# Layer 0 of a four-layer graph network: the two key blocks of exp added on VectorE ahead of the products with ones, with new rows of turns

## The chip, the cores and the metric

The kernel runs on one core of a Trainium2 chip. The metric is device time in microseconds (us), the median of several executions. The kernel before takes 2660.74 us (median of 3 runs, 2660.52 to 2662.13).

In the profile PE is TensorE's matmul, PEld its weight load, DVE is VectorE, ACT is ScalarE, POOL is GpSimd and SP is SyncE.

## The reference, cut to what matters

64 graphs of 256 nodes with 256 features go through four attention layers, each with a residual and a norm. The change is in layer 0, masked softmax attention with four heads of 64 features:

```python
x, adj                       # (64, 256, 256) each
q, k, v = proj(Wq, bq), proj(Wk, bk), proj(Wv, bv)        # 4 heads of 64
attn = einsum('bhnd,bhmd->bhnm', q, k) * 64 ** -0.5
attn = where(adj == 0, -1e9, attn)
attn = softmax(attn, axis=-1)
out = einsum('bhnm,bhmd->bhnd', attn, v)
out = out.reshape(B, 256, 256) @ Wo.T + bo
x = layernorm(x + layernorm(out) * gamma + beta)
# layer 1: 8 heads of 32 without projections, then a feed-forward of 1024 with gelu
# layers 2 and 3: one head each, edge scores with leaky_relu
```

The kernel works on groups of two graphs, 32 groups in all. It holds exp of the scores with the keys on the partitions, in two blocks of 128 keys. A sum over all keys is a sum over the partitions of both blocks.

## The kernel before: the parts that count here

All groups are Python generators. One turn of a group records the instructions up to its next `yield`; each row of turns is a string of digits that says which group comes next. `FIRST` starts the pipeline, `ORDER` is one period of the steady part (a digit is how many periods ago a group began), and `LAST` ends it. On TensorE the order of the program is kept.

```python
ORDER = "011225334342343542234235432323132121321132121"
...
    att = ctx.enter_context(tc.tile_pool(name="att", bufs=2))
    ps_s = ctx.enter_context(tc.tile_pool(name="ps_s", bufs=2, space=bass.MemoryType.PSUM))
    ps_m = ctx.enter_context(tc.tile_pool(name="ps_m", bufs=4, space=bass.MemoryType.PSUM))
...
    def scores(i, cs, qT, kT, mask, hd, scale, sums=None):
        m = P // hd
        es = []
        for c in cs:
            pss = [ps_s.tile([P, 2, QB * N], F32, name="ps") for _ in range(m // 2)]
            ...  # matmuls of kT and qT into pss
            for ps in pss:
                e = att.tile([P, 2, QB * N], F32, name="e", bufs=6)
                nc.scalar.activation(e, ps, AF.Exp, scale=scale)                      # L605
                if sums is None:      # layer 0
                    nc.vector.tensor_tensor(e, e, mask..., ALU.mult)                  # L607
                else:                 # layer 1: product with the mask, and its sum
                    ... nc.vector.scalar_tensor_tensor(..., accum_out=...)            # L613
                es.append(e)
        return es

    def products(i, cs, v, es, hd, oT, sums, gamma, tally):
        po = ps_m.tile([P, len(cs), N], F32, name="pm")
        ...  # matmuls of v and e into po
        if gamma is not None:
            ...                       # layer 1 ends here
            return
        pz = ps_m.tile([P, N], F32, name="pm")
        for kc in range(QB):
            for h in range(4):
                matmul(pz[32 * h:32 * h + 32, :], ones[:, 0:32], es[h // 2][:, h % 2, kc * N:(kc + 1) * N],
                       start=kc == 0, stop=kc == QB - 1)
        nc.scalar.copy(oT, po)                                                        # L640
        nc.vector.reciprocal(sums, pz)                                                # L641, sums is zs
        nc.scalar.activation(pz, sums, AF.Copy, accum_out=tally[i])                   # L642
```

`attention` runs `scores` of a step, then `products` of the step before. In layer 0 a step is one graph. What comes behind the attention of layer 0:

```python
        def behind(i, oT, rz):
            ...  # rz goes through DRAM into rr, one row for each half of the partitions
            yield
            nc.vector.tensor_tensor(oT, oT, rr, ALU.mult)                             # L730
            yield
            pm = ps_m.tile([P, QB, D], F32, name="pm")
            ...  # matmuls of oT and woT into pm
            nc.vector.tensor_tensor(y[...], pm, over_blocks(bop, QB), ALU.add)        # L737
            ...
```

Beside it, of other groups: `nc.gpsimd.tensor_tensor(x, x, over_blocks(beta0), ALU.add)` (L717) in layer 0, after x has been transposed on TensorE; `transpose(pt[...], e[...], ident)` into a `ps_m` buffer in layer 3 ("ident,qT" in the profile; e has the name qT there), copied by ScalarE (L878); the transposes of xb ahead of the first feed-forward product, copied by ScalarE with scale and bias (L586).

Of the kernel before, what the change touches and what calls it, by code (L numbers as in the profile page):

```python
# [8 lines left out]
F32 = mybir.dt.float32  # L9
# [4 lines left out]
ALU = mybir.AluOpType  # L14
AX = mybir.AxisListType

P = 128
N = 256
# [3 lines left out]
QB = N // P  # L22
# [11 lines left out]
AT_ONCE = 3  # L34


ORDER = "011225334342343542234235432323132121321132121"


FIRST = "000000011000002131100110101000000101"  # L40
LAST = ("001142322312324311231243212120210102100210100031121201213200120132100101010120100010101102"
        "01021000001000010010000")
PREPARE = 2


# [355 lines left out]
def usual_input(ctx: ExitStack, tc: tile.TileContext, a: dict, out: bass.AP, flag: bass.AP):  # L401
# [7 lines left out]
    nc = tc.nc  # L409
# [5 lines left out]
    att = ctx.enter_context(tc.tile_pool(name="att", bufs=2))  # L415
# [14 lines left out]
    ones = const.tile([P, P], F32, name="ones")  # L430
# [88 lines left out]
    def in_order(ins):  # L519

        if on_pe:
            tc.add_manual_dep(ins.ins, on_pe.pop(),
                              mybir.DependencyInfo(mybir.DependencyClass.NoSync, mybir.DependencyReason.DATA),
                              reason="the order of the program")
        on_pe.append(ins.ins.name)

    def matmul(*args, **kw):
        in_order(nc.tensor.matmul(*args, **kw))  # L528
# [60 lines left out]
    def scores(i, cs, qT, kT, mask, hd, scale, sums=None):  # L589

        m = P // hd
        es = []
        for c in cs:
            pss = [ps_s.tile([P, 2, QB * N], F32, name="ps") for _ in range(m // 2)]
            for kc in range(QB):
                for h in range(m):
                    r = h * hd
                    matmul(pss[h // 2][:, h % 2, kc * N:(kc + 1) * N],  # L600
                           kT[r:r + hd, c, i * N + kc * P:i * N + (kc + 1) * P],
                           qT[r:r + hd, c, i * N:(i + 1) * N], start=True, stop=True)
            for ps in pss:
                e = att.tile([P, 2, QB * N], F32, name="e", bufs=6)
                nc.scalar.activation(e, ps, AF.Exp, scale=scale)  # L605
                if sums is None:
                    nc.vector.tensor_tensor(e, e, mask.unsqueeze(1).to_broadcast([P, 2, QB * N]), ALU.mult)  # L607
                else:
                    for h in range(2):
                        for kc in range(QB):  # L610
                            k = slice(kc * N, (kc + 1) * N)
                            j = 2 * len(es) + h
                            nc.vector.scalar_tensor_tensor(e[:, h, k], e[:, h, k], 1.0, mask[:, k], ALU.mult, ALU.mult,  # L613
                                                           accum_out=sums[:, kc, c, j:j + 1])
                es.append(e)
        return es

    def products(i, cs, v, es, hd, oT, sums, gamma, tally):

        m = P // hd
        po = ps_m.tile([P, len(cs), N], F32, name="pm")
        for n, c in enumerate(cs):
            for kc in range(QB):
                for r in range(0, P, 32):
                    h = r // hd
                    e = es[n * (m // 2) + h // 2]
                    matmul(po[r:r + 32, n, :], v[:, i * QB + kc, c * P + r:c * P + r + 32],  # L630
                           e[:, h % 2, kc * N:(kc + 1) * N], start=kc == 0, stop=kc == QB - 1)
        if gamma is not None:
            nc.scalar.activation(oT[:, cs[0], :], po[:, 0, :], AF.Identity, scale=gamma[:, cs[0]:cs[0] + 1])
            return
        pz = ps_m.tile([P, N], F32, name="pm")
        for kc in range(QB):
            for h in range(4):
                matmul(pz[32 * h:32 * h + 32, :], ones[:, 0:32], es[h // 2][:, h % 2, kc * N:(kc + 1) * N],
                       start=kc == 0, stop=kc == QB - 1)
        nc.scalar.copy(oT, po)  # L640
        nc.vector.reciprocal(sums, pz)  # L641
        nc.scalar.activation(pz, sums, AF.Copy, accum_out=tally[i])  # L642

    def attention(qT, kT, v, mask, hd, gamma, behind, tally=None):

        scale = hd ** -0.5
        m = P // hd
        before = sums = None  # L650
        after = []

        def go_on():
            for r in list(after):
                if next(r, END) == END:
                    after.remove(r)

        for i in range(G):
            for cs in ((0, 1),) if m == 2 else ((0,), (1,)):
                if cs[0] == 0 and gamma is not None:  # L660
                    sums = small.tile([P, QB, NC, 4], F32, name="r1")
                es = scores(i, cs, qT, kT, mask[:, i, :], hd, scale, sums)
                if before:
                    products(*before)
                go_on()
                if cs[0] == 0:
                    oT = att.tile([P, NC, N], F32, name="oT")
                    zs = att.tile([P, N], F32, name="zs") if sums is None else sums
                if before and before[1][-1] == NC - 1:
                    after.append(behind(before[0], before[5], before[6]))  # L670
                before = (i, cs, v, es, hd, oT, zs, gamma, tally)
                yield
        products(*before)
        after.append(behind(G - 1, oT, zs))
        yield
        while after:
            go_on()
            yield
# [22 lines left out]
    def layer0(g, x, mask):  # L701
# [20 lines left out]
        def behind(i, oT, rz):  # L722
# [26 lines left out]
            yield  # L749

        yield from attention(qT, kT, v, mask, 64, None, behind, [r_0[:, g * G + i:g * G + i + 1] for i in range(G)])
        return xb, z

    def layer1(xb, z, mask):
# [6 lines left out]
        def behind(i, oT, r):  # L761
# [14 lines left out]
            yield  # L776

        yield from attention(zT, zT, z, mask, 32, gamma1, behind)
        yT = transposed(xb, gamma2, beta2)
        yield  # L780
# [212 lines left out]
    def turn(g):  # L993
        done[g] += 1
        next(groups[g], END)
        if g == 0 and done[0] > PREPARE:
            next(preparing, END)

    for g in FIRST:
        turn(int(g))  # L1000
    for period in range(len(groups)):
        for age in ORDER:
            g = period - int(age)
            if g >= 0:
                due[g] += 1
                if due[g] > done[g]:
                    turn(g)
    for back in LAST:
        turn(len(groups) - 1 - int(back))
# [55 lines left out]
```

## Time and profile before

| what | value |
|---|---|
| time, median of 3 | 2660.74 us |
| span of the profiled execution | 2659.6 us |
| mean granted clock of TensorE | 0.992 |
| instructions | 44925 |
| mean rate of memory traffic | 31 GB/s |
| PE waits in the whole span, behind DVE z (L559) | 8.2 us in 30 waits, longest 0.3 |
| PE waits behind DVE oT (L730) | 8.6 us in 2 waits, longest 7.0 |
| PE waits behind ACT e (L605) at the scores | 6.5 us in 5 waits, longest 4.7 |

A row of the groups names line, engine, operation, output and inputs, shapes and count; then busy time and the mean of one in ns, and the idle time ahead of it with what ended that. "x1024" counts records: an f32 product has two records on TensorE. A row of the timeline gives start and duration in us, and in brackets the idle time ahead of it. Busy times of groups whose instructions run beside each other are the time they cover together.

### The profile page before, as it was taken

How to read it: one execution, taken by the hardware profiler on the slowest of the kernel's cores; microseconds unless marked ns; L12 is line 12 of the kernel's file. 1: busy time of each engine (PE TensorE's matmuls, PEld its weight loads, DVE VectorE, ACT ScalarE, POOL GpSimd, SP SyncE). 2: the span in 40 equal slices, each digit the busy share in tenths (PEclk: the TensorE clock that was granted, in tenths of full speed). 3: DMA queues.
4: the chain of work that ended last, by engine and by line, in shares of the span. 5: the costliest groups of instructions: out<-in, count | busy, mean ns of one | idle time of the engine just before them, and what ended most of it. 6: DMA issues, size and time to landing. Idle time of an engine off the chain costs nothing.

```text
span 2659.6 us, 44925 instructions
## 1 busy us (share of the span) xinstructions
PE 2586.6 (97%) x16648; PEld 1765.4 (66%) x16648; DVE 1967.4 (74%) x6189; ACT 1290.4 (49%) x1995; POOL 586.8 (22%) x1139
## 2 busy tenths in 40 slices
PE   6899999999999999999999999999999999999997
PEld 3467667666667676666676666676676676676665
DVE  4667777777777777777777777777777777777774
ACT  3445544545544445545455444555445455445442
POOL 1112222212222212222222222222222222222121
PEclk8999999999999999999999999999999999999998
DMA  5000011000010100110010110010110001000000
GB/s 155 25 9 29 29 37 30 31 29 29 29 37 28 33 30 26 32 37 26 28 37 25 32 37 25 29 37 21 36 37 25 29 29 29 29 29 17 17 1 25
DMA packets 113729, 83.20 MB, mean 31 GB/s; under 512 B 44256, under 2 KB 113120, under 8 KB 113504
## 3 DMA queue, kind: packets, MB, share of 16 engines
q1 hardware_dynamic: 112144, 79.47, 9.8%
q8 instruction: 134, 2.20, 0.3%
q10 hardware_dynamic: 1360, 0.79, 0.1%
q14 instruction: 91, 0.75, 0.1%
HBM read 54.80 MB, written 17.04 MB: 27 GB/s over the span
## 4 chain that ended last, share of the span: by engine, by line
PE 70%; DVE 17%; POOL 8%; issue 2%; DMA 1%; SPq 1%; ACT 1%; DVEq 0%; POOLq 0%; ACTq 0%
PE pm L528 54%; PE ps L528 10%; PE pm L531 7%; POOL rstd L551 6%; DVE st L544 3%; DVE y L814 2%; DVE y L742 2%; DVE xn L559 2%; POOL ve L547 2%; DVE z L559 2%; DVE mv L545 1%; DVE xb L748 1%; DVE y L741 1%; DVE r L813 1%; POOL ve L549 0%
## 5 line engine op out<-in xcount | busy, mean ns | idle before, releaser
L613 DVE SCALAR_TENSOR_TENSOR e<-e,mask 128x256 f32<-128x256 f32 x1024 | 428.3, 483 | 129.0 <-ACT e L605 129.0
L605 ACT ACTIVATE e<-ps 128x1024 f32<-128x1024 f32 x384 | 372.0, 1019 | 196.6 <-PE ps L528 176.3
L528 PE MATMUL pm<-L_gnn_W,hT 128*128 128x256 f32 x2048 | 463.2, 380 | 0.0
L528 PE MATMUL pm<-xT,L_gnn_W 128*128 128x512 f32 x1024 | 456.4, 594 | 0.0
L528 PEld LDWEIGHTS pm<-L_gnn_W,hT 128*128 128x128 f32 x2048 | 385.3, 191 | 48.9 <-issue 1.1
L786 ACT ACTIVATE hT<-pm,b 128x512 f32<-128x512 f32 x256 | 176.7, 690 | 409.8 <-PE pm L528 409.8
L528 PEld LDWEIGHTS pm<-xT,L_gnn_W 128*128 128x128 f32 x1024 | 193.0, 191 | 204.0 <-issue 199.5
L544 DVE BATCH_NORM_STATS2 st<-y 128x6 f32<-128x256 f32 x768 | 301.1, 408 | 6.7
L551 POOL TENSOR_TENSOR rstd<-ve,mhalf 128x2 f32<-128x2 f32 (+1 forms) x384 | 297.7, 775 | 26.6
L559 DVE TENSOR_SCALAR xn<-y,mv,rstd 128x256 f32<-128x256 f32 x384 | 142.2, 412 | 177.3 <-POOL rstd L551 177.3
L547 POOL TENSOR_SCALAR ve<-mv 128x2 f32<-128x2 f32 x384 | 98.7, 257 | 750.4 <-DVE mv L545 749.9
L772 POOL TENSOR_TENSOR both<-y,xb 128x512 f32<-128x512 f32 x64 | 81.3, 1270 | 757.2 <-DVE y L771 757.2
L607 DVE TENSOR_TENSOR e<-e,mask 128x1024 f32<-128x1024 f32 x128 | 151.0, 1220 | 18.5 <-ACT e L605 18.5
L528 PE MATMUL ps<-xT 32*128 32x256 f32 x2048 | 147.5, 401 | 2.2 <-ACT e L605 1.3
L586 ACT ACTIVATE xT<-pm,beta,gamma 128x512 f32<-128x512 f32 x128 | 92.2, 769 | 108.4 <-PE pm L531 108.3
L528 PE MATMUL pm<-e,z 128*32 128x256 f32 x2048 | 141.5, 385 | 0.4
L528 PEld LDWEIGHTS ps<-xT 32*128 32x128 f32 x2048 | 93.1, 184 | 73.3 <-issue 67.1
L528 PE MATMUL ps<-qT,kT 64*128 64x256 f32 x1024 | 129.2, 392 | 5.2 <-ACT e L605 5.2
L528 PE MATMUL pm<-e,v 128*32 128x256 f32 x2048 | 126.4, 387 | 6.3 <-DVE e L607 6.3
L528 PE MATMUL pm<-L_gnn_WoT,oT 128*128 128x256 f32 x512 | 119.3, 387 | 8.6 <-DVE oT L730 8.6
L528 PE MATMUL pm<-xT,L_gnn_WqT 128*128 128x512 f32 x256 | 121.2, 617 | 3.5 <-ACT xT L584 3.5
L814 DVE SCALAR_TENSOR_TENSOR y<-pm,r,xn 128x256 f32<-128x256 f32 x256 | 120.8, 473 | 2.5
(136 smaller groups left out, 4053.7 us busy)
## 6 DMA issues: line engine op xcount, KB each, us to landing
x<-in_x SPq DMA_DIRECT2D x32, 512.0 KB
adj<-in_adj SPq DMA_DIRECT2D x32, 512.0 KB
rr<-lines SPq DMA_DIRECT2D x128, 128.0 KB
out<-xn SPq DMA_DIRECT2D x31, 512.0 KB
adjT<-adjb SPq DMA_TRANSPOSE x128
L_gnn_W<-in_L_gnn_W SPq DMA_DIRECT2D x2, 1024.0 KB
lines<-zs SPq DMA_DIRECT2D x64, 4.0 KB
out<-xn SPq DMA_DIRECT2D x2, 256.0 KB
```

The costliest lines, as they stand in the source:

```text
L528: in_order(nc.tensor.matmul(*args, **kw))
L531: in_order(nc.tensor.transpose(*args))
L544: nc.vector.bn_stats(st[:, q, :], src[:, t, 0:D])
L547: nc.gpsimd.tensor_scalar(ve[:, 0], mv[:, :, 1], EPS, None, ALU.add)
L551: nc.gpsimd.tensor_tensor(rstd, ve, mhalf[:, 0:k * QB].rearrange("p (k t) -> p k t", k=k), ALU.pow)
L559: nc.vector.tensor_scalar(dst[:, t, 0:D], src[:, t, 0:D], mv[:, q, 0:1], rstd[:, q:q + 1], ALU.subtract, ALU.mult)
L586: nc.scalar.activation(dst[:, c, on], pt[:, on], AF.Identity, bias=bias[:, c:c + 1], scale=scale[:, c:c + 1])
L605: nc.scalar.activation(e, ps, AF.Exp, scale=scale)
L607: nc.vector.tensor_tensor(e, e, mask.unsqueeze(1).to_broadcast([P, 2, QB * N]), ALU.mult)
L613: nc.vector.scalar_tensor_tensor(e[:, h, k], e[:, h, k], 1.0, mask[:, k], ALU.mult, ALU.mult, accum_out=sums[:, kc, c, j:j + 1])
L786: nc.scalar.activation(hT[:, f, :], pm, AF.Gelu, bias=b1[:, f:f + 1])
L814: nc.vector.scalar_tensor_tensor(y[:, t, :], po[:, 0:D], r, x[:, t, 0:D], ALU.mult, ALU.add)
```

## The change

Layer 0's exp of both key blocks is added on VectorE, and TensorE multiplies that sum with ones, so that it has half as many products with ones. The additions have four buffers of their own. The rows of turns are others. The change is meant to move work from TensorE to VectorE.

```diff
-ORDER = "011225334342343542234235432323132121321132121"
+ORDER = "012215233434324354232423432321325321231112312"
-FIRST = "000000011000002131100110101000000101"
-LAST = ("001142322312324311231243212120210102100210100031121201213200120132100101010120100010101102"
-        "01021000001000010010000")
+FIRST = "0000000001100013110011010120020000011"
+LAST = ("011041222323213243212131321121042101200012010030112121021320102012101010310010102001010102"
+        "101010002000100010001000")
...
-        es = []
+        es, added = [], []
...
                 if sums is None:
                     nc.vector.tensor_tensor(e, e, mask.unsqueeze(1).to_broadcast([P, 2, QB * N]), ALU.mult)
+                    both = att.tile([P, 2, N], F32, name="ee", bufs=4)
+                    nc.vector.tensor_tensor(both, e[:, :, 0:N], e[:, :, N:QB * N], ALU.add)
+                    added.append(both)
...
-        return es
+        return es, added
...
         pz = ps_m.tile([P, N], F32, name="pm")
-        for kc in range(QB):
-            for h in range(4):
-                matmul(pz[32 * h:32 * h + 32, :], ones[:, 0:32], es[h // 2][:, h % 2, kc * N:(kc + 1) * N],
-                       start=kc == 0, stop=kc == QB - 1)
+        for h in range(4):
+            matmul(pz[32 * h:32 * h + 32, :], ones[:, 0:32], added[h // 2][:, h % 2, :], start=True, stop=True)
```

More of the change, by code (lines that the diff above doesn't have):

```diff
@@ L615, in scores, with products @@
                 es.append(e)
-        return es
-    def products(i, cs, v, es, hd, oT, sums, gamma, tally):
+        return es, added
+    def products(i, cs, v, es, hd, oT, sums, gamma, tally, added):
         m = P // hd
@@ L661, in attention @@
                     sums = small.tile([P, QB, NC, 4], F32, name="r1")
-                es = scores(i, cs, qT, kT, mask[:, i, :], hd, scale, sums)
+                es, added = scores(i, cs, qT, kT, mask[:, i, :], hd, scale, sums)
                 if before:
@@ L670, in attention @@
                     after.append(behind(before[0], before[5], before[6]))
-                before = (i, cs, v, es, hd, oT, zs, gamma, tally)
+                before = (i, cs, v, es, hd, oT, zs, gamma, tally, added)
                 yield
```

## Prediction

> **What bounds the kernel now.** I read the busy shares first, then the stages, then one period of the steady part engine by engine.
>
> ```profile
> PE 2586.6 (97%) x16648; PEld 1765.4 (66%) x16648; DVE 1967.4 (74%) x6189; ACT 1290.4 (49%) x1995; POOL 586.8 (22%) x1139
> ```
>
> ```profile
> 1200.00:1600.00 400.00, 398.31 (x2598) 273.48 (x2597) 303.96 (x953) 200.37 (x309) 91.33 (x175) 1.00 0.10 31
> ```
>
> In the stage table the columns are window, length, then busy time of PE, weight loads, DVE, ACT, POOL, clock, DMA share, GB/s. In the middle PE idles 1.7 of 400 us; of its 73 us of idle time 36 lie in the first 133 us (133 less 41.53 and 55.07) and 25 in the last 133. The chain that ended last repeats every 80.3 us (the same piece starts at 1299.28 and 1379.59), one group of two graphs, so PE idles 0.34 us per group, nearly all of it one 0.28 us wait for z. PE bounds the middle, in program order: a wait on PE is lost time unless an earlier one made room.
>
> What the change touches, in the groups kept apart by shape:
>
> ```profile
> L607 DVE TENSOR_TENSOR e<-e,mask 128x1024 f32<-128x1024 f32 x128 | 151.0, 1220 | 18.5 <-ACT e L605 18.5
> L641 DVE RECIPROCAL zs<-pm 128x256 f32<-128x256 f32 x64 | 111.9, 1749 | 6.0 <-PE pm L528 1.6
> L528 PE MATMUL pm<-e,ones 128*32 128x256 f32 x1024 | 68.0, 382 | 0.0
> L771 DVE TENSOR_TENSOR y<-y,xb 128x512 f32<-128x512 f32 x64 | 42.9, 670 | 1.1
> ```
>
> The timeline of one period (start, duration) shows where they stand. PE, with the weight loads left out:
>
> ```profile
> 1367.23 2.00 PE L528 MATMUL ps<-qT,kT 64*128 64x256 f32 x16
> 1369.16 1.09 PE L531 MATMUL pm<-ident,xn 128*128 128x128 f32 x8
> 1370.18 1.07 PE L528 MATMUL pm<-e,z 128*32 128x256 f32 x16
> 1371.18 2.00 PE L528 MATMUL ps<-qT,kT 64*128 64x256 f32 x16
> 1373.11 1.93 PE L528 MATMUL pm<-e,v 128*32 128x256 f32 x32
> 1374.86 1.05 PE L528 MATMUL pm<-e,ones 128*32 128x256 f32 x16
> 1375.84 0.66 PE L531 MATMUL pm<-ident,oT 128*128 128x128 f32 x4
> 1376.42 1.93 PE L528 MATMUL pm<-e,v 128*32 128x256 f32 x32
> 1378.17 1.05 PE L528 MATMUL pm<-e,ones 128*32 128x256 f32 x16
> 1379.15 0.44 PE L531 MATMUL pm<-ident,qT 128*128 128x128 f32 x2
> ```
>
> DVE and ACT beside it:
>
> ```profile
> 1370.59 2.35 DVE L607 TENSOR_TENSOR e<-e,mask 128x1024 f32<-128x1024 f32 x2
> 1373.46 2.36 DVE L607 TENSOR_TENSOR e<-e,mask 128x1024 f32<-128x1024 f32 x2 [0.52 <-ACT e L605]
> 1375.97 1.76 DVE L641 RECIPROCAL zs<-pm 128x256 f32<-128x256 f32 x1
> ```
>
> ```profile
> 1377.82 0.39 ACT L642 ACTIVATE pm<-zs 128x256 f32<-128x256 f32 x1 [2.07 <-DVE zs L641]
> 1378.15 0.19 ACT L642 ACTIVATION_READ_ACCUMULATOR pm<-zs 128x1 f32 x1
> ```
>
> The built program says what the qT transposes at 1379.15 wait for: the tally of the first graph (L642), because they take the PSUM buffer that its sums of exp held. It ends at 1378.34, so 0.81 us are to spare. That slack is what I think the change uses up.
>
> **What the Trainium skill says.** "TensorE: Matmul & The Clock Gate", section "Part 3: Packing small matmuls — row/col tiling": small tiles of the array work at the same time. The trace agrees: 16 records of the products with ones, 382 ns each, take 0.98 us of PE. "VectorE: DVE Perf Modes", "The perf-mode tier table": a tensor_tensor in f32 has only the single rate, 2293 ns for 2048 elements; the trace has 670 ns for 512, and I use that. "SBUF — State Buffer", "Who interferes with whom": a VectorE instruction with two SBUF inputs contends with a GpSimd instruction that reads SBUF, and the later one fully blocks. The trace agrees:
>
> ```profile
> 1346.39 2.42 POOL L717 TENSOR_TENSOR x<-x,beta 128x1024 f32<-128x1024 f32 x1 [2.97 <-PE pm L531]
> 1346.53 0.08 DVE L613 DVE_READ_ACCUMULATOR e<-e,mask 128x1 f32 x1
> 1346.53 2.56 DVE L613 SCALAR_TENSOR_TENSOR e<-e,mask 128x256 f32<-128x256 f32 x1
> ```
>
> The L613 beside GpSimd's addition takes 2.56 us; its neighbours take 0.42.
>
> **The change part by part.**
>
> *Removed.* A graph's products with ones go from 8 to 4, 16 records to 8: 0.98 to 0.49 us of PE. Per group 0.98 us, over 32 groups 31 us.
>
> *Added.* 128 additions of 128x512 on DVE, about 0.67 us each: 86 us, 2.7 us per group. DVE then has some 64 us of an 80 us period, so as a sum it fits. The place matters. Set t = 0 at the first graph's scores (1367.23). In the new program DVE runs multiply, add, multiply, add, then the same for the second graph, and only then the first graph's reciprocal.
>
> The second graph's exp is ready at t = 6.2, as now (1373.46). A multiply lasts 1.22 us and its addition follows at once; the next multiply starts about 0.60 us after that (the start-to-start step of L730, likewise 128x512). So: multiply 6.23, add 7.48, multiply 8.09, add 9.34, reciprocal 9.95. Before, the reciprocal started at 8.74. Its tally starts 1.85 us after it (1375.97 to 1377.82) and lasts 0.52: it ends at 12.32. PE meanwhile arrives at the qT transposes 0.98 us sooner, at 11.92 - 0.98 = 10.94. It waits about 1.4 us, where it had 0.81 to spare: more than the saving.
>
> The products stay fed: the second e is due at t = 9.5 on PE and done at 9.3, the last sum due at 10.6 and done at 10.0.
>
> *Moved by the rows of turns.* In the steady part three blocks change places on PE. The projection to k moves behind layer 1's third products, which leaves DVE 3.6 us more before the scores at t = 0; useful, but the chain above starts at ACT's exp and gains nothing. The output projection of layer 0 now stands behind the first four W1 products: that covers the reciprocals that come late, but W1 now follows the ex transposes directly. Its xT comes from ACT, which in the timeline starts two L586 at 7.97 us after the qT transposes and needs 0.77 for the first, so it is there at 8.74; PE is there at 8.60. That is a wait of some 0.2 us.
>
> The third is the transposes of the next x. They now stand between the first and second scores of layer 1, and one W2 block behind the first products of layer 1, so only 4.5 us of PE work (x 0.87, the row 0.2, one W2 block 3.46) and scores (1.08) divide the first scores from those products, which start 6.7 us after the first scores do. GpSimd's x + beta starts once these transposes and the rstd before it are done: 2.95 us after the scores, until 5.37. DVE's first multiplication starts at 3.2 us (exp is ready 3.15 us after the scores now). It meets the addition and ends near 5.65; seven more at 0.345 us end at 8.07. The products need the seventh at 7.07 and have it at 7.8. I put 0.6 us of wait on this.
>
> *Sum per group:* -0.98 + 1.4 + 0.2 + 0.6 = +1.2 us, the wait for z as it is. Over some 29 steady groups: +35 us, 2696. The first and last rows are new too; I did not work them out and allow 5 us either way.
>
> **Rivals.** (1) *The saving comes through.* PE is the bound and the rows were redone to hide DVE's work: 2661 - 31 = about 2630. For it: 97% on PE, and DVE idle for 19 us of each period. Against it: the chain exp, two multiplies and two additions, reciprocal, tally, transposes has no slack left, and none of its steps is moved by the rows. (2) *Only the PSUM buffer holds:* the waits at W1 and at layer 1's products do not come about. Then it is -0.98 + 1.4 = +0.4 per group, about 2674. (3) *DVE becomes the bound:* 64 of 80 us and some 16 us of waiting for GpSimd's rstd would leave no room; stalls at z and xn as well, 2715 and over. Against it: those waits stand where I found the same distances as before.
>
> I choose between the main sum and rival 2, nearer the first, and leave room for the saving.
>
> **Range and chances.** 2690 us, 2648 to 2712 in 8 of 10. Faster by over 2% would need 53 us, more than all the PE time removed: 0.02. Slower by over 2% (2714) needs rival 3: 0.08. Within 2%: 0.90.
>
> **What would show it.** Right: the period near 81.4 us in the chain; among PE's waits the qT transposes behind ACT's tally of zs, about 1.4 us some 30 times; the reciprocal 1.2 us later after the scores; one L613 of over 2 us in the first set of layer 1, with a PE wait of 0.6 us for e; products with ones at 512 records and 34 us. Wrong: a period below 80 us, or no wait ahead of the qT transposes. That would mean that the buffer comes free in another way than I read, or that DVE overlaps the additions more closely than L730 and L771 do.

## The result, and the profile after

The changed kernel takes 2709.15 us (median of 4 runs, 2708.08 to 2713.64), the kernel before in the same session 2661.43 us (2660.52 to 2664.07): 1.0181 times as long, interval 1.0163 to 1.0198. The prediction was 2690 us within 2648 to 2712. Direction and mechanism held; the loss is 48 us where the steps summed to 35, and the time lies only 3 us inside the upper end of the range.

Line numbers in the changed kernel are higher by one to four: the multiplication is L608 (L607 before), the addition is L610, layer 1's product with the mask is L617 (L613), the reciprocal of the sums L643 (L641), its tally L644 (L642), GpSimd's x + beta L719 (L717).

The busy shares of the changed kernel, from its page:

```profile
PE 2594.9 (96%) x16136; PEld 1751.4 (65%) x16136; DVE 2071.9 (77%) x6317; ACT 1285.5 (47%) x1995; POOL 582.3 (22%) x1139
```

Its stage table for the same 400 us as before (window, length, busy time of PE, weight loads, DVE, ACT, POOL, clock, DMA share, GB/s):

```profile
1200.00:1600.00 400.00, 391.76 (x2459) 263.86 (x2457) 313.68 (x966) 193.58 (x300) 87.31 (x172) 1.00 0.10 30
```

DVE has 105 us more in the whole span. PE idles 8.2 of 400 us instead of 1.7, which is 1.7 us per group instead of 0.34. The same piece of the chain now starts every 82.04 us:

```profile
750.84 8.04 PE pm L528 x28
832.88 8.04 PE pm L528 x28
```

A group is 1.73 us longer than the 80.30 before; 29 groups make 50 us, so the whole loss lies in the steady part, and the first and last rows gave some 3 us back. The shares of the chain by engine have turned too:

```profile
PE 51%; DVE 30%; POOL 8%; ACT 6%; issue 4%; DMA 1%; SPq 1%; ACTq 0%; DVEq 0%; POOLq 0%
```

PE's part was 70% and VectorE's 17%. A longer part of the path now runs over VectorE.

The groups that the change touches, kept apart by shape:

```profile
L608 DVE TENSOR_TENSOR e<-e,mask 128x1024 f32<-128x1024 f32 x128 | 156.1, 1221 | 16.8 <-ACT e L606 12.7
L643 DVE RECIPROCAL zs<-pm 128x256 f32<-128x256 f32 x64 | 111.9, 1749 | 0.0
L610 DVE TENSOR_TENSOR ee<-e 128x512 f32<-128x512 f32 x128 | 88.2, 691 | 4.1
L528 PE MATMUL pm<-ee,ones 128*32 128x256 f32 x512 | 39.3, 379 | 0.0
```

The additions cost 88.2 us, 691 ns each. The reciprocal used to find DVE idle ahead of it for 6.0 us in all; now for none, so it always queues behind other VectorE work. The products with ones fell from 1024 records and 68.0 us to 512 and 39.3.

PE's waits in the whole span (us in total, times, longest us):

```profile
PE pm L531 <- ACT pm L644: 36.5, 29, 1.5
```

This one is new, once per group; the wait for z is what it was (7.9 us in 29 waits). PE's timeline where the new wait stands:

```profile
1386.05 2.00 PE L528 MATMUL ps<-qT,kT 64*128 64x256 f32 x16
...
1394.81 1.93 PE L528 MATMUL pm<-e,v 128*32 128x256 f32 x32
1396.56 0.61 PE L528 MATMUL pm<-ee,ones 128*32 128x256 f32 x8
1398.43 0.44 PE L531 MATMUL pm<-ident,qT 128*128 128x128 f32 x2 [1.25 <-ACT pm L644]
1398.70 3.80 PE L528 MATMUL pm<-xn,qT 128*128 128x257 f32 x16
1402.34 3.67 PE L528 MATMUL pm<-wx,xT 128*128 128x259 f32 x16
```

DVE beside it, from the second graph's exp to the second reciprocal:

```profile
1392.29 1.23 DVE L608 TENSOR_TENSOR e<-e,mask 128x1024 f32<-128x1024 f32 x1
1393.55 0.69 DVE L610 TENSOR_TENSOR ee<-e 128x512 f32<-128x512 f32 x1
1394.16 1.22 DVE L608 TENSOR_TENSOR e<-e,mask 128x1024 f32<-128x1024 f32 x1
1395.41 0.69 DVE L610 TENSOR_TENSOR ee<-e 128x512 f32<-128x512 f32 x1
1396.02 1.75 DVE L643 RECIPROCAL zs<-pm 128x256 f32<-128x256 f32 x1
...
1398.96 1.75 DVE L643 RECIPROCAL zs<-pm 128x256 f32<-128x256 f32 x1
```

And ACT with the first graph's tally:

```profile
1397.87 0.39 ACT L644 ACTIVATE pm<-zs 128x256 f32<-128x256 f32 x1 [3.29 <-DVE zs L643]
1398.19 0.19 ACT L644 ACTIVATION_READ_ACCUMULATOR pm<-zs 128x1 f32 x1
```

The chain can be read off these three: multiply, add, multiply, add without a gap, the reciprocal 9.97 us after the first graph's scores (1396.02 less 1386.05), the tally done at 1398.38, and 0.05 us later the qT transposes start.

The second loss shows in no wait of PE. PE in layer 1, same kernel:

```profile
1364.27 1.15 PE L528 MATMUL ps<-xT 32*128 32x256 f32 x16
1365.35 1.86 PE L528 MATMUL pm<-e,z 128*32 128x256 f32 x16
1367.14 3.72 PE L528 MATMUL pm<-L_gnn_W,hT 128*128 128x256 f32 x16
```

The same 16 records of products took 1.07 us before, and 1.00 us from their start to that of the next row; now it is 1.79. No bracket says that PE idled. What happens on DVE and on GpSimd at that time:

```profile
1361.68 2.34 DVE L617 SCALAR_TENSOR_TENSOR e<-e,mask 128x256 f32<-128x256 f32 x1 [1.38 <-ACT e L606]
...
1363.95 0.41 DVE L617 SCALAR_TENSOR_TENSOR e<-e,mask 128x256 f32<-128x256 f32 x1
```

```profile
1361.38 2.35 POOL L719 TENSOR_TENSOR x<-x,beta 128x1024 f32<-128x1024 f32 x1
```

One product with the mask takes 2.34 us where its neighbour takes 0.41, exactly while GpSimd adds beta. The later ones start 0.345 us apart, and the matmuls of the products are issued as each of them is done: the wait lies between the records of one row and is counted as busy. The records themselves are no longer than before (388 ns on average, 385 before), they start further apart. TensorE's weight loads do list this wait, and two more that PE's list lacks:

```profile
PEld pm L528 <- DVE e L617: 37.0, 103, 0.7
PEld pm L528 <- ACT xT L586: 19.8, 62, 0.5
PEld pm L528 <- ACT pm L644: 10.4, 30, 1.7
```

Before, the first two had 5.7 and 0.5 us, and there was no third. The second is W1 waiting for xT; the third is layer 3's products with xn waiting for the tally of the second graph.

From starts to starts, a group has these differences from before: ones of the first graph 0.55 us instead of 0.98; ones of the second graph with the wait behind them 1.87 instead of 0.98; layer 1's first products 1.79 instead of 1.00; W1 behind the ex transposes 0.67 instead of 0.48, and its own stride 3.53 instead of 3.43; layer 3's products with xn 3.64 instead of 3.46; transposes of x 0.93 instead of 0.87. Blocks that only have other neighbours now: two W2 blocks 3.55 and 3.65 instead of 3.45 and 3.55, and the projection to k 3.44 instead of 3.63. That sums to +1.79 us, against +1.73 in the period.

### The profile page after: what moved, and what is told of

The parts are those of the page before. It is cut to its first block, busy times and chain, and to the rows that moved or that the text cites. A ratio compares the mean times of both kernels' runs of the same rounds, so it can differ in the third digit from the quotient of the medians.

```text
span 2706.5 us, 43749 instructions
## 1 busy us (share of the span) xinstructions
PE 2594.9 (96%) x16136; PEld 1751.4 (65%) x16136; DVE 2071.9 (77%) x6317; ACT 1285.5 (47%) x1995; POOL 582.3 (22%) x1139
## 4 chain that ended last, share of the span: by engine, by line
PE 51%; DVE 30%; POOL 8%; ACT 6%; issue 4%; DMA 1%; SPq 1%; ACTq 0%; DVEq 0%; POOLq 0%
PE pm L528 41%; POOL rstd L551 6%; PE ps L528 6%; DVE e L617 5%; PE pm L531 4%; DVE st L544 3%; DVE e L608 3%; DVE zs L643 2%; ACT e L606 2%; DVE y L816 2%; DVE y L744 2%; DVE xn L559 2%; POOL ve L547 2%; DVE xb L750 2%; DVE z L559 1%
## 5 line engine op out<-in xcount | busy, mean ns | idle before, releaser
L617 DVE SCALAR_TENSOR_TENSOR e<-e,mask 128x256 f32<-128x256 f32 x1024 | 422.2, 475 | 144.6 <-ACT e L606 143.1
L559 DVE TENSOR_SCALAR xn<-y,mv,rstd 128x256 f32<-128x256 f32 x384 | 163.8, 467 | 83.1 <-POOL rstd L551 83.1
L608 DVE TENSOR_TENSOR e<-e,mask 128x1024 f32<-128x1024 f32 x128 | 156.1, 1221 | 16.8 <-ACT e L606 12.7
L528 PE MATMUL pm<-e,z 128*32 128x256 f32 x2048 | 163.5, 388 | 2.4
L528 PE MATMUL pm<-v,qT 128*128 128x260 f32 x512 | 119.3, 386 | 2.9 <-DVE qT L845 1.8
L528 PE MATMUL pm<-xn,qT 128*128 128x257 f32 x512 | 121.4, 386 | 0.1
```

Source lines behind the costliest of these rows:

```text
L559: nc.vector.tensor_scalar(dst[:, t, 0:D], src[:, t, 0:D], mv[:, q, 0:1], rstd[:, q:q + 1], ALU.subtract, ALU.mult)
```

## The experiments

The theory: the loss has two independent parts. The *additions* put the first graph's reciprocal and tally behind two more additions, and the qT transposes wait for the PSUM buffer (+0.5 to +0.6 us per group, saving included). The *new rows* put GpSimd's x + beta onto layer 1's first products, and W1 right behind the transposes that feed it (+1.1). The rivals: the rows cost nothing and the additions all of it (through VectorE as a whole); or the buffer alone holds PE.

### The rows alone

The kernel before with the new three strings of turns, and nothing else:

```diff
-ORDER = "011225334342343542234235432323132121321132121"
+ORDER = "012215233434324354232423432321325321231112312"
... # FIRST and LAST likewise
```

> The kernel before with the new rows of turns alone, no additions. Theory (three places of waiting, two of them made by the rows): layer 1's first products still wait about 0.8 us for a multiplication held up by GpSimd's x + beta, W1 still waits 0.2 to 0.3 us for xT; the qT transposes do not wait. So +1.2 us per group, about 2696 us. Rival (only the additions on VectorE cost, the rows are neutral or help): 2661 us or less.

Measured: 2703.49 us, 1.015 times before (1.0133 to 1.0167; before 2664.56). The period, from the chain, is 81.44 us (1407.99 to 1489.43), +1.13 per group without a single addition. Layer 1's first products are stretched just as in the changed kernel:

```profile
1366.58 1.86 PE L528 MATMUL pm<-e,z 128*32 128x256 f32 x16
1368.37 3.72 PE L528 MATMUL pm<-L_gnn_W,hT 128*128 128x256 f32 x16
```

So two thirds of the loss per group (1.13 of 1.73) comes from the rows. The rival in which the additions cost all of it is out. In time the rows alone lose 39 us, more than 29 times 1.13: the steady part of this kernel began at 186.5 us, that of the changed kernel at 176.6.

### The additions with the old rows

The changed kernel with the three strings of before.

```diff
-ORDER = "012215233434324354232423432321325321231112312"
+ORDER = "011225334342343542234235432323132121321132121"
... # FIRST and LAST likewise
```

> The changed kernel with the rows of turns of before. Theory: no wait at W1 or at layer 1's first products; but VectorE's first multiplication starts at 3.4 us after the first scores instead of 2.3, so that the reciprocal starts at 10.8 and the qT transposes wait about 2.2 us in all (a part of it may show at the products with v). 0.98 us saved, +1.2 us net per group, about 2698 us. Rival (the rows are what costs): below 2661, down to 2632 us.

Measured: 2711.78 us, 1.018 (1.0163 to 1.0197). Most periods are 81.75 to 81.77 us; some are up to 82.05, and the mean of 26 is 81.85, +1.55. PE in one of them:

```profile
1404.07 1.07 PE L528 MATMUL pm<-e,v 128*32 128x256 f32 x16 [0.38 <-DVE e L608]
...
1407.07 0.44 PE L531 MATMUL pm<-ident,qT 128*128 128x128 f32 x2 [1.49 <-ACT pm L644]
```

Here a further wait comes in: the multiplications behind the additions are late for the products with v, 32 times, 13.9 us in all. In the new rows that wait is gone from the steady part. This is what the new rows save: with them the additions cost +0.60 (82.04 less 81.44), with the old ones +1.55. But they take 1.13 for it, so that both sets of rows end within a few us of each other.

### GpSimd's x + beta left out

The changed kernel without the addition of layer 0's beta to x, which is left out of the computation altogether:

```diff
-        nc.gpsimd.tensor_tensor(x, x, over_blocks(beta0), ALU.add)
```

> The changed kernel without GpSimd's addition of beta0 to x, which is left out (beta0 is all zeros in these inputs). Theory (that addition blocks VectorE's first multiplication of layer 1): no multiplication of over 2 us, and layer 1's first products run in 1.0 us instead of 1.8; 0.9 us per group less, about 2683 us. Rival (those products wait for exp or for VectorE's list, not for GpSimd): no change, 2705 us or more.

Measured: 2691.18 us, 1.0095 (1.0078 to 1.0112); period 81.25, 0.79 less than with it. Layer 1's first products, on PE:

```profile
1444.17 1.07 PE L528 MATMUL pm<-e,z 128*32 128x256 f32 x16
```

The row is back to 1.07 us, and 0.79 is just what it had been stretched by; the weight loads' wait for these multiplications falls from 37.0 to 7.2 us. The W2 block behind them still takes 3.65 us, so its 0.10 is a matter of its place. The wait of the qT transposes is untouched (36.4 us, 29 times). The two parts are independent, and the stretched row was a wait for VectorE, which waited for GpSimd.

The same on the other side: the kernel before with the new rows, and this addition kept, but done on VectorE.

```diff
-        nc.gpsimd.tensor_tensor(x, x, over_blocks(beta0), ALU.add)
+        nc.vector.tensor_tensor(x, x, over_blocks(beta0), ALU.add)
```

> The new rows alone without any addition of the key blocks, and the addition of beta0 to x on VectorE instead of GpSimd. Theory (most of what the rows cost is GpSimd's addition in the way of layer 1's first multiplication): 0.8 to 0.9 us of the 1.13 us per group vanish, period about 80.6 us, about 2678 us. Rival (the other changes of place cost as much): 2690 us or more.

Measured: 2678.5 us, 1.005 (1.0035 to 1.0066; before 2665.16); period 80.65, again 0.79 below that of the rows alone. At its new place on VectorE the addition costs PE nothing. The 0.35 us left over the kernel before is W1's place (0.29) and the transposes of x (0.06).

### A shorter reciprocal

The changed kernel, with the reciprocal over half of the queries; the other half of the sums is replaced by 1, so half of layer 0's softmax stays undivided.

```diff
-        nc.vector.reciprocal(sums, pz)
+        nc.gpsimd.memset(sums[:, N // 2:N], 1.0)
+        nc.vector.reciprocal(sums[:, 0:N // 2], pz[:, 0:N // 2])
```

> The changed kernel with the reciprocal of the sums taken for half of the queries only; the other half is set to one by GpSimd, so that half of layer 0's softmax is left undivided. The reciprocal takes 0.9 us instead of 1.75. Theory (the reciprocal stands in that chain, ahead of the tally and of the layer-1 result): PE's wait ahead of the qT transposes falls from 1.4 to about 0.5 us, and 0.2 us behind it vanish; 1.0 us per group less, about 2679 us. Rival (the waits are set by something else, as the copy that freed the buffer and gained nothing would suggest): 2705 us or more.

Measured: 2680.31 us, 1.0064 (1.0048 to 1.0079; before 2663.65); period 81.08, 0.96 less. PE's waits:

```profile
PE pm L531 <- ACT pm L645: 13.9, 29, 0.7
```

The reciprocal takes 0.95 us instead of 1.75, and the wait fell from 36.5 to 13.9 us in all, 0.78 each; the products with xn behind the transposes, which waited for the tally of the second graph, are back to 3.46 us, another 0.18. The reciprocal is on the path with its full length.

### The additions done twice

```diff
                     nc.vector.tensor_tensor(both, e[:, :, 0:N], e[:, :, N:QB * N], ALU.add)
+                    nc.vector.tensor_tensor(both, e[:, :, 0:N], e[:, :, N:QB * N], ALU.add)
```

> The changed kernel with each addition done twice (the second writes the same sum again). Theory (VectorE's list from the first exp to the layer-1 result behind the reciprocal is the chain that PE waits for): two more additions delay the second graph's multiplications by 1.0 us and two more stand behind them, so the reciprocal starts 2.2 us later and PE loses that in every group, about 2770 us. Rival (VectorE has 16 us of idle time per period and 2.4 us more are hidden): below 2720 us.

Measured: 2816.07 us, 1.0574 (1.0557 to 1.059). That is 107 us over the changed kernel, for 88 us of further additions, and more than the 2770 I expected. PE in one period:

```profile
1537.00 1.07 PE L528 MATMUL pm<-e,v 128*32 128x256 f32 x16 [0.53 <-DVE e L608]
...
1540.42 0.62 PE L528 MATMUL pm<-ee,ones 128*32 128x256 f32 x4 [1.93 <-DVE ee L611]
...
1541.25 5.32 PE L528 MATMUL pm<-xn,qT 128*128 128x257 f32 x16
```

What I had missed: once VectorE is late enough, the products wait for it too, not only the buffer. The ones wait 1.93 us for their sum, the products with v 0.53 for a multiplication. The periods are 84.48 and 86.17 us in turn. In the longer ones the products with xn take 5.16 us from start to start, in the others 3.47, and here it is not a wait: the granted clock of TensorE was lower. The two rows, with the columns of the stage table (the clock is third from the end):

```profile
1456.77:1460.24 3.47, 3.47 (x19) 3.04 (x18) 3.46 (x8) 0.88 (x3) 1.24 (x1) 1.00 0.24 81
1541.25:1546.41 5.16, 5.16 (x19) 4.22 (x18) 3.59 (x8) 0.88 (x3) 1.27 (x1) 0.67 0.16 52
```

At a clock of 0.67, 5.16 us are worth 3.46 at full clock, which is all of the difference. So the waits cost 2.44 us per group (84.48 less 82.04), near the 2.2 that I expected, for four further additions of 0.67 us: hardly any of them is hidden. The lower clock adds 0.85 us per group on average, and the steady part began at 187.0 us instead of 176.6; over 29 groups these three make 106 us. Why the clock fell there was not tested.

### The buffer freed at once

If only the PSUM buffer holds PE, a copy of the sums into SBUF by ScalarE frees it before the reciprocal:

```diff
-        nc.vector.reciprocal(sums, pz)
-        nc.scalar.activation(pz, sums, AF.Copy, accum_out=tally[i])
+        zc = att.tile([P, N], F32, name="zc")
+        nc.scalar.copy(zc, pz)
+        nc.vector.reciprocal(sums, zc)
+        nc.scalar.activation(zc, sums, AF.Copy, accum_out=tally[i])
```

> The changed kernel, but ScalarE copies the sums of exp from PSUM into SBUF at once, and reciprocal and tally work on the copy, so that the PSUM buffer comes free before them. Theory (the buffer held through reciprocal and tally is what the qT transposes wait for): that wait of 1.4 us and 0.2 us at the products behind it vanish; 1.5 us per group less, about 2664 us. Rival (VectorE's longer list is the cost, whoever holds the buffer): the wait shows up elsewhere, 2700 us or more.

Measured: 2711.66 us, 1.0178 (1.0161 to 1.0195). I had expected some 45 us off; there was none. PE:

```profile
1400.82 0.44 PE L531 MATMUL pm<-ident,qT 128*128 128x128 f32 x2
1402.17 3.71 PE L528 MATMUL pm<-xn,qT 128*128 128x257 f32 x16 [0.91 <-DVE y L772]
```

DVE:

```profile
1399.74 1.74 DVE L645 RECIPROCAL zs<-zc 128x256 f32<-128x256 f32 x1
1401.40 0.62 DVE L772 TENSOR_TENSOR y<-pm,r 128x512 f32<-128x512 f32 x1
```

The transposes no longer wait, and the products right behind them wait instead: their PSUM buffer is read by L772, which stands in VectorE's queue behind the same reciprocal. 26.5 us in 29 waits have taken the place of 36.5. The Trainium skill, "PSUM — Partial Sum Buffer", section "Engine vs sequencer instructions", says that VectorE's queue is strictly first in, first out; the trace agrees, L772 starts at 1401.40, as the reciprocal's 1.74 us end. So my explanation by the buffer was too narrow. What is late is VectorE's list in order, and whatever PE needs behind it waits in turn.

The period did fall, to 81.70, by 0.34: the additions cost 0.26 us per group over the rows alone instead of 0.60. That the time did not fall is a matter of start and end. The regular pieces of the chain begin at 184.18 us instead of 176.61, the first of them is 1.3 us longer (granted clock 0.85 in it, 1.00 in that of the changed kernel), and the end takes 2 more: together they use up 29 times 0.34. In the first 190 us the wait for oT has 8.5 us instead of 2.2, but the wait for layer 0's e 2.1 instead of 7.8, so the waits don't tell why the start differs; the granted clock of the first 176 us was 0.92 instead of 0.94. The cause was not settled.

### Versions that might beat both

First graph of a group only, with the new rows, and x + beta on VectorE: half of the saving, two additions fewer ahead of the reciprocal.

```diff
+                    if i == 0:
                         both = att.tile([P, 2, N], F32, name="ee", bufs=4)
                         nc.vector.tensor_tensor(both, ...)
... # products: i == 0 takes the sums, i == 1 both blocks as before
-        nc.gpsimd.tensor_tensor(x, x, over_blocks(beta0), ALU.add)
+        nc.vector.tensor_tensor(x, x, over_blocks(beta0), ALU.add)
```

> The new rows, with additions for the first graph of a group only, whose two fit into the time in which VectorE waits for the second graph's exp; the second graph keeps its eight products with ones. The addition of beta0 to x is done by VectorE instead of GpSimd, in the gap before the second scores of layer 1. Theory: no wait ahead of the qT transposes, none at layer 1's first products, half of the saving on PE (0.49 us): period 81.43 - 0.85 - 0.49 = 80.1 us, about 2654 us, below both kernels. Rival (any addition on VectorE costs more than it saves): 2665 us or more.

Measured: 2667.2 us, 1.0013 (1.0006 to 1.0019; before 2663.65). Both waits are gone and the period is 80.24, 0.06 below before: most of the 0.43 us saved on ones is taken back by W1's place (0.29) and the transposes of x (0.06). The period is near the expected 80.1 and the time is 13 us above the expected 2654; the steady part began at 187 us instead of 177.

So back to the old rows, which have no such cost. There the first graph's additions would meet layer 1's scaling of xb on VectorE; an order between two VectorE instructions puts this scaling behind the first addition.

```diff
... # old ORDER, FIRST, LAST; additions for i == 0 only; x + beta on GpSimd
+                        sums_made.append(nc.vector.tensor_tensor(both, ...).ins.name)
...
+                if sums_made and i == 0:
+                    tc.add_manual_dep(ins.ins, sums_made[-2], ...)    # ins: the scaling of xb
```

> The rows of turns of before, additions for the first graph of a group only, and VectorE told to do layer 1's xb of the first graph behind the first addition instead of ahead of the multiplications (an order on one engine, no wait). Theory (only what stands behind the second graph's exp in VectorE's list costs): the second graph's first multiplication starts 0.4 us later, the tally ends 0.1 us after PE reaches the qT transposes; 0.49 us saved per group, 0.1 given back, about 2652 us against 2663. Rival (any addition costs what it saves): 2660 us or more.

Measured: 2662.78 us, 0.9996 (0.9987 to 1.0004; before 2663.38), period 80.20. No difference: the products with xn take 3.81 us from start to start instead of 3.46, so most of the 0.43 is lost once more behind VectorE: the weight loads of these products wait 14.3 us in all for the tally of the second graph.

> As the run beside it, but with one addition per group (two of the first graph's four heads). Theory: multiplication, addition, multiplication and the two xb end at 6.0 us after the first scores, before the second graph's exp is ready at 6.2; nothing is delayed and PE has a quarter of the saving, 0.245 us per group: about 2655.5 us against 2663. Rival: 2660 us or more.

This one is the same with a single addition per group (the first two heads of the first graph; `if i == 0 and not es`). Measured: 2664.54 us, 1.0002 (0.9994 to 1.0011), period 80.29. The expected quarter of the saving did not come, and no wait took it: the products with xn are at 3.47 us. The products with ones are no shorter:

```profile
1378.24 0.39 PE L529 MATMUL pm<-ee,ones 128*32 128x256 f32 x2
...
1378.47 0.82 PE L529 MATMUL pm<-e,ones 128*32 128x256 f32 x6
1379.22 0.66 PE L532 MATMUL pm<-ident,oT 128*128 128x128 f32 x4
```

Their 12 records take 0.98 us (1378.24 to 1379.22), as 16 did before; 8 records, one product for each of the four heads, take 0.55. With two heads left at two products each, PE has nothing saved, so this run says only that one addition costs PE nothing in this place.

Last, the version with both additions of the first graph (2662.78 us), together with the copy of the sums to SBUF, which had not lowered the time of the changed kernel:

```diff
+        zc = att.tile([P, N], F32, name="zc")
+        nc.scalar.copy(zc, pz)
-        nc.vector.reciprocal(sums, pz)
+        nc.vector.reciprocal(sums, zc)
... # and the tally on zc
```

> The version with additions for the first graph only and xb behind the first addition, rows of before, and with ScalarE's copy of the sums of exp into SBUF, so that reciprocal and tally hold no PSUM buffer. Theory (without the copy PE waited 0.35 us at the products of layer 3 for the second graph's tally): that wait goes, and the half saving of 0.49 us per group stands; period 79.8 to 79.9 us, about 2650 us against 2663. Rival (VectorE's list gives out elsewhere, at the products with wx): 80.2 us, 2660 us or more.

Measured: 2655.41 us (2653.71 to 2655.58), 0.9963 (0.995 to 0.9977; before 2665.16). It is faster than both kernels, 0.4% against the kernel before. The period is 79.88, 0.42 below before, and the removed work is 0.43. PE:

```profile
1376.82 0.44 PE L532 MATMUL pm<-ident,qT 128*128 128x128 f32 x2
1377.10 3.63 PE L529 MATMUL pm<-xn,qT 128*128 128x257 f32 x16
1380.57 3.66 PE L529 MATMUL pm<-wx,xT 128*128 128x259 f32 x16
```

DVE:

```profile
1370.62 0.41 DVE L788 TENSOR_SCALAR xb<-y,mv,rstd 128x256 f32<-128x256 f32 x1
1370.95 0.68 DVE L612 TENSOR_TENSOR ee<-e 128x512 f32<-128x512 f32 x1
1371.55 0.41 DVE L788 TENSOR_SCALAR xb<-y,mv,rstd 128x256 f32<-128x256 f32 x1
1371.87 2.35 DVE L609 TENSOR_TENSOR e<-e,mask 128x1024 f32<-128x1024 f32 x2
1374.16 1.75 DVE L653 RECIPROCAL zs<-zc 128x256 f32<-128x256 f32 x1
```

Without the second graph's additions the reciprocal starts 8.83 us after the first graph's scores (1374.16 less 1365.33), 0.09 later than before instead of 1.2. With the list on VectorE short enough, the last thing that held PE (0.34 us at the products with xn, 3.81 to 3.47) was the buffer of the sums, and the copy frees it. The copy in the kernel before, without additions, was not run; its trace has nothing for it to gain, as the qT transposes had 0.81 us to spare there and the products with xn took 3.46.

## Why the prediction was right, and where its sizes were off

**PE bounds the middle in program order; a saving there is lost to waits.** This was right. PE has 29 us less work with ones (68.0 less 39.3), and the kernel takes 48 us more.

**The chain exp, multiplies, additions, reciprocal, tally, transposes.** This was right to a few hundredths. Predicted were the reciprocal at 9.95, the tally done at 12.32 and a wait of about 1.4 us; measured were 9.97, 12.33 and 1.25 us listed. The products with ones fell by 0.43 us per graph, not 0.49. Ones and wait are together 0.46 us longer per group (0.55 + 1.87 less twice 0.98), where -0.98 + 1.4 gives 0.42. The Trainium skill names this pattern in "Perfetto Trace Analysis", section "Optimization Strategy": the same gap repeating on the engine that should be saturated can mean too little SBUF or PSUM for the next tile. This trace agrees as far as the gap goes, 29 times 1.25 us, but the copy to SBUF shows that the buffer was only about half of the cause (0.34 of 0.60 us). The rest was VectorE's order: layer 1's result stands behind the reciprocal too, and PE needs it next. The prediction did not see that.

**GpSimd's x + beta against layer 1's first multiplication.** This was right in place and mechanism: I put DVE's first one 3.2 us after the scores and its end at 5.65; it ran from 3.18 to 5.52 (1361.68 and 1364.02 less 1358.50). The Trainium skill, "SBUF — State Buffer", section "Who interferes with whom", says that the later of the two fully blocks, and 2.34 us beside 0.41 agree. The size was off: 0.6 us predicted, 0.79 measured. And I expected to find it among PE's waits; it is among those of the weight loads.

**W1 behind the ex transposes.** This was right; 0.2 us was predicted, 0.19 came in the gap and 0.10 more in the stride of the first W1 products.

**What the sum missed.** Layer 3's products with xn (+0.18), which wait for the second graph's tally and which the half reciprocal frees, and the transposes of x (+0.06) are not in it. Of its own terms the most mis-sized is layer 1's first products (0.79 for 0.6: +0.19); W1 adds 0.09 and the chain 0.04. The two W2 blocks (+0.20) and the projection to k (-0.19) cancel. Together that is 0.57 us, for the 0.51 by which a group exceeds the +1.22 that the terms make. None is large. The prediction worked out where a wait begins, and not what stands right behind it.

**The number.** 2690 was put below the sum of 2696, to leave room for the saving. The room was needed on the other side: 2709 is inside the range by a narrow margin.

**First and last rows, allowed 5 us either way.** They gave some 3 us back in this case. But kernels with the same rows began their steady part between 176 and 187 us, so the allowance was too narrow.

**The rivals.** That the saving comes through is out, since the period is above 80. That only the buffer holds (2674) is out, since the rows alone cost 1.13 us per group. VectorE is not the bound in the changed kernel, with 314 of 400 us; the additions done twice show such waits beginning, with PE waiting for the sums themselves.

## What to carry to other kernels

Before moving work to an engine with idle time, follow what that engine already has queued behind the new work, and how much slack each of those has until the bound engine needs it: 19 us idle per period did not help, 0.81 us of slack decided. When the schedule is changed to make room, time the new schedule without the change; here it made two thirds of the loss per group. Move only the part of the work that fits the slack, and free the buffer that would hold the bound engine as well. Here the smaller move gained nothing without the copy, the copy took no time off the changed kernel, and the two together gave 0.4%.

## What was not expected of the hardware

A wait between the matmuls of one row of products does not show as idle time of PE: the row's time goes from 1.07 to 1.86 us and PE counts as busy. It shows in start-to-start times against the kernel before, and in the waits of the weight loads (37.0 us for L617, 5.7 before). Of the some 2.6 us that a group loses in the changed kernel (1.73 in the period and 0.86 that the shorter products with ones had saved), PE's idle time has 1.35. A PE busy share of 96% hides the rest.

A stretched row is not always a wait. With the additions done twice a row of 3.47 us took 5.16 in every other period, at a granted clock of 0.67.

Twelve records of products with ones, two heads with one product and two with two, took the 0.98 us of sixteen; eight, one for each head, took 0.55. The head with the most products set the time in these three cases.

The time until the steady part differed by 11 us between kernels with the same rows (176.2 with the half reciprocal, 176.6 for the changed kernel, 187.1 with additions for the first graph only). The granted clock of the first 176 us was 0.94 in the first two and 0.90 in the third, which makes at most some 7 of the 11 us (0.04 of 176); whether the clock or the waits came first was not tested. So a few us in the total can hide a change of the period or feign one; the period in the chain is the finer measure.

The reciprocal costs the same from PSUM (1749 ns) and from SBUF (1744 ns).
